# A two-layer graph network on one core: the DMAs that fold the exponentials move from SyncE's queue to ScalarE's

## The chip, the cores and the metric

The kernel runs on one core of one Trainium2 chip. The time is that of the device for one launch, in microseconds (us). The core has five engines with a stream of instructions each: TensorE (PE in the profile; its weight loads are PEld), VectorE (DVE), ScalarE (ACT), GpSimd (POOL) and SyncE (SP). A DMA is issued by an instruction in the stream of one engine, and moves its data on the core's 16 DMA engines.

## The reference

There are 128 graphs of 128 nodes each, with 256 features per node, and for each graph a matrix of zeros and ones, `adj`. Layer 0 is attention with 8 heads whose values depend on the relation, here 0 or 1, followed by a feed-forward network with GELU. Layer 1 has two steps of graph attention and a feed-forward network with ReLU. Layer norms stand between. What matters here is the attention of layer 0:

```python
scores = jnp.einsum('bhid,bhjd->bhij', q, k) / np.sqrt(dh)
attn = jax.nn.softmax(scores, axis=-1)
out = jnp.zeros_like(q)
for r in range(Wv.shape[0]):
    v_r = (src @ Wv[r] + bv[r]).reshape(Bb, Nn, h, dh).transpose(0, 2, 1, 3)
    mask = (adj_matrix == r)[:, None]
    out = out + jnp.einsum('bhij,bhjd->bhid', attn * mask, v_r)
```

The softmax needs a sum of exponentials over the source nodes for each head and each target node, and the change lies in the making of this sum.

## The kernel before, in words

**Tiling.** The 16,384 nodes are worked on in 32 groups of 512, that is 4 graphs. All data are 32-bit. In attention a group is two pairs of graphs, p = 0 and p = 1. A tile `e` holds the exponentials of a pair: the 128 partitions are source nodes, and the free dimension runs over 4 head positions `s` (4 of the 8 heads, each for two column halves `c`), the pair's 2 graphs, 2 halves and 128 targets. Each head position is one block of 128 x 512.

**The order of the work** is written out by hand. The strings FRONT, STEADY and TAIL are lists of tokens; `d:1` runs the next step of the generator `folded` for the group after the base, `a` steps attention, `f` and `k` the first and second feed-forward network, `fc` and `kc` a chain of each of them, `q` the projections, `n`, `t` norms and transposes, `l` layer 1. FRONT covers the start and parts of the first three groups, STEADY is repeated for each base group 1 to 29, and TAIL ends the run. Each engine takes its own instructions strictly in this order. So a period of the steady part holds work of several groups: pair 1 of one group's attention stands beside the second feed-forward network of the group two before.

**The steps around the change.** `scores` (L859) makes four banks of scores by matmul, and four instructions on ScalarE turn them into `e` (L866). DVE multiplies `e` by `adj` into the tile `pm` (L875). `sums` multiplies `e` and `pm` by the values, into `pav` (L929), and then multiplies the folded exponentials `es` by a constant `split` into `pden` (L917). `folded`, which the diff touches, makes `es`: for each half h of the head positions two DMAs (L891) copy, within the core's own memory (SBUF), 64 partitions by 2 blocks of 256 columns: the upper 64 source nodes of the pair's first graph go beside the lower ones of the second, and the reverse. That is 128 KB per DMA, 4 DMAs per pair, 8 per group. Then ScalarE copies the halves that stay on their partitions into a part of `pm` not yet in use (L900, two copies of 64 x 512 per h), and DVE adds both (L902). Only after that may L875 write the same part of `pm`, and the last matmuls of `pav` read it.

**The generator's steps.** The first `yield` comes after the two DMAs of h = 0, the second after those of h = 1; then one after each L900 copy and each L902. So in the list of one engine the two DMAs of one h are neighbours, and other work may stand between the two h.

**Other work named in the prediction.** In the feed-forward networks TensorE accumulates in one bank, `seeded`, that ScalarE first fills with a copy of another bank (L621, L648, L650). L629 copies `seeded` out into p16 before the next product is added to it, and L584 does the same with a bank `ph7` into p7. The step T4 of TensorE is the product that adds to `ph7` after L584. L633 and L592 are DVE's sums of these copies with banks, L549 the GELU or ReLU. L806 copies out a bank of the values' projection. L465 splits rows into planes of 16 bits, SP issues a transposing DMA of them (L468), and L493 puts the result together as `yT`. SP's queue carries also the loads of x, xT and adj (L226, L237, L223), the weights (L51), the store of the output (L1083) and a spreading of a column by way of HBM (L1008, L1009).

**Queues.** SP issues all DMAs but the first five loads of small parameters, which ScalarE issues. A wait of an instruction for more than one semaphore is carried by instructions EVENT_SEMAPHORE ahead of it in the same stream.

Of the kernel before, what the change touches and what calls it, by code (L numbers as in the profile page):

```python
# [189 lines left out]
def fast_pass(ctx, tc, a, out):  # L190
# [5 lines left out]
    nc = tc.nc  # L196
# [684 lines left out]
    def folded(S):  # L881

        n = str(S["g"])
        for p in range(G // 2):
            e = S["e", p]
            S["es", p] = es = w1p.tile([P, HC, NCH * P], F32, tag="es", name=f"es_{n}_{p}")
            for h in range(2):
                hs = slice(2 * h, 2 * h + 2)
                for lo in range(2):
                    to, fr = (slice(x * P // 2, (x + 1) * P // 2) for x in (lo, 1 - lo))  # L890
                    nc.sync.dma_start(  # L891
                        es[to, hs], e[fr, hs, lo].rearrange("p s c i -> p s (c i)")
                    )
                yield
            for h in range(2):
                hs = slice(2 * h, 2 * h + 2)
                ea = S["pm", p][:, 2 + h].rearrange("p u c i -> p u (c i)")
                for lo in range(2):
                    own = slice(lo * P // 2, (lo + 1) * P // 2)
                    nc.scalar.copy(ea[own], e[own, hs, lo].rearrange("p s c i -> p s (c i)"))  # L900
                    yield
                nc.vector.tensor_add(es[:, hs], es[:, hs], ea)  # L902
                yield
# [206 lines left out]
    with tc.manual_schedule(engines={ET.PE, ET.Activation, ET.DVE, ET.SP, ET.Pool}):  # L1110
# [29 lines left out]
        def loading(ops):  # L1140
# [11 lines left out]
        )  # L1152
        by_group = dict(
            d=folded, q=lambda S: projections(S) if S["g"] < 2 else projected(S),
            a=attention, f=first_ffn, l=layer1, k=second_ffn,
            fc=lambda S: S["chain", 1], kc=lambda S: S["chain", 3],
# [377 lines left out]
```

## Time and profile before

| what | us |
|---|---|
| median of 3 runs (2633.99 to 2634.73) | 2634.33 |
| the profiled execution | 2633.71 |
| its span, first to last instruction | 2631.9 |
| TensorE busy | 2598.8 |
| DVE busy | 2246.7 |
| ScalarE busy | 1857.4 |
| one DMA of L891 on SP, median of 256 | 0.599 |
| from issue to landing of such a DMA, median | 2.4 |
| a group in the steady part, start to start | 80.1 |

The profile is of one execution. A row of groups or of a timeline has the start, the duration, the engine, the line of the kernel, the operation, the tile written and the tile read, the shape and how often it comes in a row; behind it in square brackets the time for which the engine was idle just before, and what ended that. A name with q, such as SPq or ACTq, is the sequencer of an engine, which issues DMAs and reads semaphores; such time isn't counted as busy. TensorE's clock was granted at 0.998 of full speed over the span.

### The profile page before, as it was taken

The page shows a single profiled execution, that of the slowest core. Times are in us where ns is not written, and L with a number is a line of the kernel's source. Part 1 is how long each engine was busy: PE and PEld are TensorE (multiplying, and loading weights), DVE is VectorE, ACT ScalarE, POOL GpSimd, SP SyncE. Part 2 cuts the span into 40 slices and gives each one's busy share as a digit, 9 for nine tenths or more (in the row PEclk, how much of TensorE's full clock was granted, in tenths as well). Part 3 has the DMA queues.
Part 4 walks back from the last instruction along what each step waited for, and adds up shares of the span by engine and source line. Part 5 has one row for each costly group of instructions (what it writes and reads, how often), then busy time and mean ns, then how long its engine had stood idle before and what let it go on. Part 6 is the DMA issues. An engine that isn't in the chain of part 4 may idle for free.

```text
span 2631.9 us, 54467 instructions
## 1 busy us (share of the span) xinstructions
PE 2598.8 (99%) x20842; PEld 2302.5 (87%) x20842; DVE 2246.7 (85%) x5921; ACT 1857.4 (71%) x3839; POOL 141.8 (5%) x137
## 2 busy tenths in 40 slices
PE   8999999999999999999999999999999999999997
PEld 6888898888988988988889888889889899888886
DVE  5888888889888988888988888988889888889877
ACT  4767777667677677776776776776767777767764
POOL 0000000000000000000000000000000000000000
PEclk9999999999999999999999999999999999999999
DMA  6222232232233222222322232222323222222211
GB/s 177 69 63 61 64 66 66 53 73 65 55 67 61 65 61 65 65 66 53 75 64 59 63 67 59 63 64 65 69 53 73 61 61 65 65 57 70 60 29 34
DMA packets 317371, 170.60 MB, mean 65 GB/s; under 512 B 222768, under 2 KB 295600, under 8 KB 317104
## 3 DMA queue, kind: packets, MB, share of 16 engines
q1 hardware_dynamic: 316000, 166.66, 28.0%
q8 instruction: 166, 2.72, 0.4%
q14 instruction: 101, 0.83, 0.1%
q10 hardware_dynamic: 1104, 0.40, 0.1%
HBM read 66.20 MB, written 16.90 MB: 32 GB/s over the span
## 4 chain that ended last, share of the span: by engine, by line
PE 92%; DVE 3%; DMA 2%; ACT 2%; issue 1%; SPq 0%; POOL 0%; ACTq 0%; POOLq 0%; DVEq 0%
PE po L534 16%; PE ph L525 16%; PE seeded L525 13%; PE seeded L534 12%; PE pwo L969 4%; PE pav L929 4%; PE pw L1046 4%; PE pqqa L789 4%; PE pvqa L789 4%; PE pqqb L789 3%; PE pvqb L789 3%; PE ps L859 2%; PE py L1059 2%; PE pg L1072 2%; PE pden L917 1%; DVE x L445 1%
## 5 line engine op out<-in xcount | busy, mean ns | idle before, releaser
L465 ACT COPY planes<-x 128x512 uint16<-128x512 uint16 x384 | 227.0, 617 | 161.2 <-DVE x L445 160.5
L493 ACT COPY yT<-pT 128x512 uint16<-128x512 uint16 x384 | 268.0, 764 | 63.6 <-DMA pT<-planes 63.6
L431 POOL TENSOR_TENSOR rs<-rs,mhalf 128x4 f32<-128x4 f32 x129 | 139.5, 1081 | 2430.7 <-DVE rs L430 1836.9
L525 PE MATMUL seeded<-yS,w_L_gnn_w_ff 128*128 128x256 f32 x768 | 208.8, 394 | 2.8 <-ACT seeded L621 1.6
L866 ACT ACTIVATE e<-ps 128x512 f32<-128x512 f32 x256 | 137.0, 591 | 103.1 <-issue 89.9
L525 PE MATMUL seeded<-yS,w_L_gnn_W 128*128 128x256 f32 x768 | 204.0, 388 | 1.3 <-DVE yS L505 0.9
L525 PE MATMUL ph<-yT,w_L_gnn_w_ff 128*128 128x256 f32 x768 | 201.1, 385 | 0.5 <-ACT yT L493 0.2
L525 PE MATMUL ph<-yT,w_L_gnn_W 128*128 128x256 f32 x768 | 197.1, 380 | 0.0
L407 DVE BATCH_NORM_STATS2 st<-x 128x6 f32<-128x256 f32 x512 | 190.8, 414 | 2.4
L534 PE MATMUL po<-w_L_gnn_W,hT 128*128 128x128 f32 x1536 | 187.1, 275 | 0.5 <-ACT hT L549 0.5
L534 PEld LDWEIGHTS po<-w_L_gnn_W,hT 128*128 128x128 f32 x1536 | 184.0, 192 | 3.8 <-ACT hT L549 0.6
L534 PE MATMUL po<-w_L_gnn_w_ff,hT 128*128 128x128 f32 x1536 | 186.9, 275 | 0.0
L534 PEld LDWEIGHTS po<-w_L_gnn_w_ff,hT 128*128 128x128 f32 x1536 | 183.8, 192 | 3.4
L525 PEld LDWEIGHTS seeded<-yS,w_L_gnn_w_ff 128*128 128x128 f32 x768 | 135.7, 189 | 51.3 <-ACT p L629 16.1
L875 DVE TENSOR_TENSOR pm<-e,adj 128x512 f32<-128x512 f32 x256 | 169.7, 683 | 10.3 <-ACT e L866 9.2
L525 PEld LDWEIGHTS seeded<-yS,w_L_gnn_W 128*128 128x128 f32 x768 | 140.4, 190 | 35.2 <-ACT p L629 8.3
L633 DVE TENSOR_TENSOR hT<-seeded,p 128x512 f32<-128x512 f32 x128 | 87.6, 684 | 90.6 <-PE seeded L525 87.1
L525 PEld LDWEIGHTS ph<-yT,w_L_gnn_w_ff 128*128 128x128 f32 x768 | 143.7, 191 | 23.3 <-ACT seeded L648 0.6
L525 PEld LDWEIGHTS ph<-yT,w_L_gnn_W 128*128 128x128 f32 x768 | 143.3, 190 | 18.8 <-ACT seeded L621 0.4
L900 ACT COPY pm<-e 64x512 f32<-64x512 f32 x256 | 157.6, 616 | 2.3
L629 ACT COPY p<-seeded 128x512 f32<-128x512 f32 x128 | 75.0, 586 | 97.0 <-PE seeded L525 96.7
L549 ACT ACTIVATE hT<-hT,c_L_gnn_b_ff 128x256 f32<-128x256 f32 x256 | 112.4, 498 | 34.5 <-DVE hT L633 32.3
(195 smaller groups left out, 6399.2 us busy)
## 6 DMA issues: line engine op xcount, KB each, us to landing
es<-e SPq DMA_DIRECT2D x256, 128.0 KB, 2.4
xT<-in_xT_dram SPq DMA_DIRECT2D x32, 512.0 KB, 3.9
x<-in_x_dram SPq DMA_DIRECT2D x32, 512.0 KB, 3.9
out_dram<-x SPq DMA_DIRECT2D x31, 512.0 KB, 2.9
spread<-hbm SPq DMA_DIRECT2D x61, 256.0 KB, 4.1
adj<-in_adjT_dram SPq DMA_DIRECT2D x32, 256.0 KB, 4.4
pT<-planes SPq DMA_TRANSPOSE x192, 3.1
w_L_gnn_W<-in_L_gnn_W_dram SPq DMA_DIRECT2D x8, 256.0 KB, 5.1
```

The source lines that it names most:

```text
L407: nc.vector.bn_stats(st[:, b % 2, :], S["x"][:, b, :])
L431: nc.gpsimd.tensor_tensor(rs[:, bs], rs[:, bs], k.mhalf[:, bs], op=ALU.pow)
L465: nc.scalar.copy(planes[:, :, b], words)
L493: nc.scalar.copy(o.rearrange("p (b t h) -> p h b t", b=2, h=2), pT[:, :, :, c, :])
L525: nc.tensor.matmul(bank[:, s * TH : (s + 1) * TH], wa[:, form, 0, f * P : (f + 1) * P], m, start=start and s == 0, stop=True, skip_group_c ...
L534: nc.tensor.matmul(bank[:, s * P : (s + 1) * P], m[:, f, s * P : (s + 1) * P], wb_[:, form, f, :], start=start and s + f == 0, stop=True, ...
L549: nc.scalar.activation(o[:, s], o[:, s] if src is None else src[:, s * TH : (s + 1) * TH], func, bias=ba[:, f : f + 1],)
L789: nc.tensor.matmul(bank[:, s * TH : (s + 1) * TH], *ops, start=start and s == 0, stop=True, skip_group_check=True,)
L866: nc.scalar.activation(e[:, s], pss[s], AF.Exp, scale=SCALE)
L875: nc.vector.tensor_mul(pm[:, s], S["e", p][:, s], S["ad"][:, pair(p), None, :].to_broadcast([P, 2, NCH, P]),)
L900: nc.scalar.copy(ea[own], e[own, hs, lo].rearrange("p s c i -> p s (c i)"))
L929: nc.tensor.matmul(pav[s * DH : (s + 1) * DH, u, c, :], v[:, d0 : d0 + DH], m[:, s, u, c, :], start=(r == 0), stop=(r == 1),)
```

## The change

In `folded` the four DMAs of a pair are issued by ScalarE in place of SP. Sizes, sources, destinations and the place in the written order stay the same.

```diff
@@ -888,7 +888,7 @@
                 hs = slice(2 * h, 2 * h + 2)
                 for lo in range(2):
                     to, fr = (slice(x * P // 2, (x + 1) * P // 2) for x in (lo, 1 - lo))
-                    nc.sync.dma_start(
+                    nc.scalar.dma_start(
                         es[to, hs], e[fr, hs, lo].rearrange("p s c i -> p s (c i)")
                     )
                 yield
```

The streams of TensorE, DVE and GpSimd hold the same instructions in the same order as before. In SP's stream the 256 issues are gone. In ScalarE's stream they stand where the written order puts them. In 29 of the 32 groups it reads, for pair 0:

```
L866 (third and fourth exponential), L650, L891 x2, L806, L891 x2, L900 x4, L806
```

and for pair 1:

```
L866 (third and fourth exponential), L891 x2, L629, L891 x2, L584, L900 x2, L549 x2, L900 x2
```

The first two DMAs of a pair wait for the second exponential, the other two for the fourth. In the first two groups and the last, and in pair 0 of the third, the neighbours differ: copies of v and yh, activations of qT, or L621 stand behind the DMAs.

## The prediction

> **What bounds the kernel now.** I read the page's busy shares and its chain first, then a table of busy time by stretch, then everything at L891, then the timeline of one steady period, engine by engine.
>
> ```profile
> PE 2598.8 (99%) x20842; PEld 2302.5 (87%) x20842; DVE 2246.7 (85%) x5921; ACT 1857.4 (71%) x3839; POOL 141.8 (5%) x137
> ...
> PE 92%; DVE 3%; DMA 2%; ACT 2%; issue 1%; SPq 0%; POOL 0%; ACTq 0%; POOLq 0%; DVEq 0%
> ```
>
> ```profile
> 0.00:75.00 75.00, 65.92 (x572) 46.03 (x576) 46.48 (x127) 39.56 (x74) 3.33 (x9) 1.00 0.71 188
> ...
> 480.00:560.00 80.00, 80.00 (x649) 71.39 (x648) 69.68 (x184) 57.90 (x121) 4.21 (x5) 1.00 0.29 64
> ```
>
> TensorE (third column of the table) sets the end, and in the steady part it has no gap: one group of 512 tokens takes 80.1 us. So whatever makes TensorE wait there is paid in full; ScalarE idles 22 us per group, but only idle time in the right place can hide anything.
>
> The 256 fold DMAs are issued by SP, which nobody else waits for at that moment:
>
> ```profile
> L891 SPq DMA_DIRECT2D es<-e x256: 590/599/2017, 17.6 to 2488.2; - x128
> ```
>
> Pair 1 of a group (p = 1), where the order puts the fold among the second feed-forward's steps (start, duration, engine):
>
> ```profile
> 1283.79 0.57 ACT L621 COPY seeded<-ph 128x512 f32<-128x512 f32 x1
> 1283.87 2.76 SPq L891 DMA_DIRECT2D es<-e  x4
> ...
> 1284.27 1.09 ACT L866 ACTIVATE e<-ps 128x512 f32<-128x512 f32 x2
> ...
> 1285.63 0.59 ACT L629 COPY p<-seeded 128x512 f32<-128x512 f32 x1 [0.27 <-PE seeded L525]
> ...
> 1286.12 0.59 ACT L584 COPY p<-ph 128x512 f32<-128x512 f32 x1
> ...
> 1286.60 1.25 ACT L900 COPY pm<-e 64x512 f32<-64x512 f32 x2
> ...
> 1288.60 1.24 ACT L900 COPY pm<-e 64x512 f32<-64x512 f32 x2
> ...
> 1289.92 0.68 DVE L902 TENSOR_TENSOR es<-es,pm 128x512 f32<-128x512 f32 x1
> ...
> 1290.64 0.69 DVE L875 TENSOR_TENSOR pm<-e,adj 128x512 f32<-128x512 f32 x1
> ```
>
> See that ScalarE runs from 1285.63 without a gap until a 1.13 us pause at 1296.5, and that the second L900 copies end at 1289.84, the DVE addition L902 starts at 1289.92, and L875 after it ends at 1291.33. TensorE reaches pav<-pm (L929) at 1291.29, and the wait it carries there ends at 1291.4: this chain already stands on TensorE's edge, with no slack.
>
> **What the Trainium skill says.** "Perfetto Trace Analysis", DMA Instruction — HWDGE: the profiled time of a DMA is time of the issuing sequencer, which is free for its next instruction only at the end; the transfer comes on top. The trace agrees: SP's four stand one after the other (2.76 us for 4), and landing is 2.4 us. "Advanced Engine Details and Errata", Sequencer Loop and Engine Queue Depths: engine instructions are queued (8 deep for ScalarE) while the sequencer goes on. The trace agrees that it runs ahead; these are L866's extra semaphore waits, read at 1278.2 to 1278.3, while two copies of yT (1278.15 to 1279.56) had yet to finish ahead of them:
>
> ```profile
> L866 ACTq EVENT_SEMAPHORE  x3: 38/38/4404, 1278.2 to 1278.3; - x3
> ```
>
> "DMA: Bandwidth & Descriptors", Issuing engines are not separate DMA queues: ScalarE's and SP's DMAs share the same 16 engines, and a second issuer saves issue time alone. No run here shows a large transfer from ScalarE.
>
> **The change part by part.**
>
> *Issue time moved onto ScalarE.* 256 x 0.6 = 154 us leave SP and come to ScalarE's sequencer, 4 per pair, 8 per group. Per DMA I take 0.64 us: 0.60 and the step to the next (four back to back take 2.63 us in pair 0). ScalarE's own five issues in the first 3 us take 0.45 to 0.49, SP's loads 0.43 to 0.47, so up to a tenth more is possible: 0.60 to 0.72.
>
> *Pair 0, 29 groups: nothing.* In the new order two DMAs follow L650, then come L806 and two more, then four L900. The first needs the second exponential, which ended at 1261.7; e three and four and L650 (until 1262.98) are queued by then and run beneath it. DMAs one and two: 1261.73 to 1263.0. L806 waits for TensorE until 1263.47 anyway. DMAs three and four: to 1264.35. L900 starts at 1264.4 in place of 1263.95, and its users L902 stand at 1266.53 and 1269.58, where two copies (to 1265.7) and four (to 1266.9) are done. The cover is L806's wait and 0.8 us on DVE; were it gone, 0.45 us per group.
>
> *Pair 1, 29 groups: the cost.* New order: both last exponentials, two DMAs, L629, two DMAs, L584. DMAs one and two need the second exponential (1283.85): 1283.87 to 1285.15, under L621 and the last exponentials. L629 still starts at 1285.63, when TensorE lets it; its extra wait is read at 1285.6 in the trace, so the sequencer stands until then. Only now DMAs three and four: 1285.68 to 1286.95, with the engine at work for 0.5 us of it and then empty. Queued behind them: L584, L900, L549 and all that follows. L584 starts at 1287.0 in place of 1286.12: 0.88 late. Who waits: the TensorE step at 1287.24 (T4) needs L584 and goes at about 1287.65, 0.4 late; L900 follows 0.88 late, so the second pair ends at 1290.72, L902 starts at 1290.77, L875 ends at 1292.18, and pav<-pm goes 0.8 to 0.85 late. T4's delay lies inside that, since it is earlier on the same path. I take 0.8. ScalarE's pause at 1296.5 then takes up its lateness; TensorE's loss stays, because its 80 us have no gap. 29 x 0.8 = 23 us. Bounds: with L629 read early, DMA three could go at 1285.40 and the loss is 0.5; with 0.72 us per DMA it is 1.0. So 15 to 29 us.
>
> *First two groups and the last.* Pairs with no L629 between: copies of v, qT or seeded lie behind up to four DMAs, 1.1 us late at 19.17, 0.5 us at 2487.04. TensorE's own waits in the first 75 us amount to 9 us and give cover. Per place from -0.5 (see next) to +1.2, six places: I take 3 us, bounds -3 to 7.
>
> *SP relieved.* SP stood with loads behind it until the exponentials came (11.4 to 17.6, 26.2 to 30.7, 37.6 to 43.6 us). Those loads go earlier; but what TensorE waits for there is named as ACT and DVE, none as a load. In steady state SP's next instructions, the transposes pT at 1272.85 and 1291.0, wait for L465, not for the fold. Nothing gained; L465 itself moves with ScalarE (0.88) and is taken up by the later TensorE. Waits that become DMAs' on ScalarE for reused semaphores concern transfers issued 20 us and more before (adj, out, x): no cost. Bytes and packets are the same.
>
> Sum on the profiled execution: its time is 2633.7 (span 2631.9 and 1.8 outside), 23 + 3 = 26 gives 2659.7; the median of the runs is 0.6 above it: 2660.
>
> **Rivals.**
>
> *A: issue and engine don't overlap* (10%): a DMA goes only when ScalarE's earlier work is finished, and holds all later. Pair 1: two DMAs 1285.4 to 1286.7, L629 1.1 late, two more after it, L584 at 1288.7, 2.6 late, pav 2.4. Pair 0: L900 2.3 late, L902 1 us, TensorE 0.4. 29 x 2.8 = 81, with 5 at the ends: 2720. Against it stands the read-ahead above.
>
> *B: hidden* (9%): later engine instructions are in the queue before the DMAs hold the sequencer, or L584 is not what decides. Then only the ends cost: 2636. Against it: program order on one queue.
>
> *C: faster* (5%): the loads freed on SP shorten the start. TensorE's named waits in the first 110 us are 7.5 us; all of them gone gives 2627. It decides only if a steady group costs under 0.08 us (7.5 less 5.3, over 29). For it: DVE waited 1.9 us there for a fold that shared the DMA engines with loads.
>
> The change does move all 128 x 2 issues, in the same place of the order, so that it does nothing is no case.
>
> **How the numbers follow.** Forecast 70%, 2648 to 2675 (15 and 29 us for the steady part, -1 to +12 for ends and a tenth dearer issue). A 10%, B 9%, C 5%; the 6% left lie between 2638 and 2648 or up to 2695. Range 2635 to 2692 takes in B's value and leaves out A, C and some spread of B: under 2 in 10. A measurement tells 0.2%, 5.3 us, from no change: faster 5% (C), same 9% (B), slower 86%.
>
> **What would show it.** In the profile after: L891 as ACTq with 0.6 us each; in a steady group L629 unmoved against TensorE's step before it, then L584 about 0.9 us later behind it (now 0.49 after L629's start); pav<-pm waiting for L875; pair 0 with L806 unmoved; a period of 80.9 us. L629 moved too, or L806, means A. A period of 80.1 means B. A longer issue than 0.72 us from ScalarE, or a wait of its DMAs for DMAs of SP, would make the sum too small.

## The result, and the profile after

| | before | after |
|---|---|---|
| median (range), us | 2634.53 (2633.99 to 2635.14) | 2691.14 (2688.45 to 2693.5) |
| the profiled execution, us | 2633.71 | 2693.5 |
| its span, us | 2631.9 | 2691.7 |
| a group in the steady part, us | 80.1 | 80.9 |
| one DMA of the fold, median us | 0.599 (SP) | 0.604 (ScalarE) |

The change makes the kernel slower: after over before is 1.0215, 95% interval [1.0201, 1.0229], or 56.6 us. The forecast was 26.

**Where the time went.** Two lines of the page, busy times and the chain that ended last:

```profile
PE 2626.0 (98%) x20842; PEld 2309.5 (86%) x20842; DVE 2253.5 (84%) x5921; ACT 1863.1 (69%) x3839; POOL 141.4 (5%) x137
...
PE 89%; DVE 3%; DMA 3%; ACT 3%; ACTq 1%; issue 1%; SPq 0%; POOL 0%; DVEq 0%; POOLq 0%
```

ScalarE does no more work than before, but its sequencer (ACTq) is now on the chain with 1%, and TensorE's share fell from 92 to 89%. TensorE's busy time rose by 27 us with the same number of instructions. The windows, cut at the same VectorE instructions in both kernels (at 150.15 and 2480.16 us before), divide this rise. Of the 27 us 10.6 lie in the start, where the clock fell from 1.00 to 0.90. Another 14.6 lie in the steady part, at a clock of 1.00 in both: there a matmul behind a wait no longer overlaps the one ahead of it, so that more of its record counts as busy. The last 2 are in the last group and behind it. The windows of the two stretches shown of before:

```profile
0.00:75.00 75.00, 54.53 (x428) 35.66 (x432) 31.04 (x80) 24.78 (x46) 2.44 (x8) 0.89 0.49 132
480.00:560.00 80.00, 79.41 (x644) 70.38 (x643) 69.50 (x183) 56.99 (x118) 4.33 (x4) 1.00 0.26 64
```

In the steady stretch TensorE lost 0.6 us of 80. In the first 75 us it ran 428 matmuls in place of 572, at a clock of 0.89 in place of 1.00. To see when the lateness arises, take one VectorE instruction after the other (their order is the same in both kernels) and subtract its start before from its start after:

| VectorE's instruction, start before (us) | 17 | 28 | 36 | 50 | 70 | 120 | 150 | 2490 | 2500 | end |
|---|---|---|---|---|---|---|---|---|---|---|
| later by (us) | 0.9 | 15.5 | 17.2 | 18.0 | 28.4 | 29.3 | 32.4 | 55.7 | 58.6 | 59.8 |

So 32 us are lost in the first 150 us, 23 in 2340 us of steady work, and 4 in the last group. The steady loss is what was forecast. The other two together were forecast with 3.

**The steady part.** Pair 1 of a group, the stretch that was shown of before (timeline of all engines: start, duration, engine):

```profile
1326.01 0.60 ACTq L891 DMA_DIRECT2D es<-e  x1
...
1327.77 0.59 ACT L629 COPY p<-seeded 128x512 f32<-128x512 f32 x1 [0.27 <-PE seeded L525]
1327.79 1.26 ACTq L891 DMA_DIRECT2D es<-e  x2
...
1329.09 0.58 ACT L584 COPY p<-ph 128x512 f32<-128x512 f32 x1 [0.73 <-ACT p L629]
1329.57 1.24 ACT L900 COPY pm<-e 64x512 f32<-64x512 f32 x2
...
1332.84 0.69 DVE L902 TENSOR_TENSOR es<-es,pm 128x512 f32<-128x512 f32 x1
1333.56 0.69 DVE L875 TENSOR_TENSOR pm<-e,adj 128x512 f32<-128x512 f32 x1
```

L629 starts at 1327.77, and only then are DMAs three and four issued, at 1327.79 for 1.26 us. L584 starts 1.32 after L629 in place of 0.49, with ScalarE idle for 0.73 us: the engine waited for its own sequencer. Everything from there to L875 is 0.8 late against L629. In TensorE's own stream the distance to the kernel before is 42.13 us until the product behind L584, 42.49 there, and 42.92 from the matmul of `pav` on that needs this L875 (1291.48 before, 1334.40 now). So the wait for L584 costs 0.36 us, in part made up, and the 0.8 us is settled at `pav`.

**The start.** ScalarE at the first fold, pair 0 of group 0:

```profile
17.35 2.06 ACT L866 ACTIVATE e<-ps 128x512 f32<-128x512 f32 x4 [1.05 <-PE ps L859]
29.27 3.58 ACTq L891 DMA_DIRECT2D es<-e  x4
32.90 0.37 ACT L737 COPY v<-pv 128x256 f32<-128x256 f32 x1 [13.48 <-DMA ga<-in_L_gnn_a_dram]
```

Before, L737 started at 19.17, right behind the exponentials. Now ScalarE is idle for 13.48 us, and the releaser that the profile names is the landing of `ga`, a load of weights that SP issued and that neither L737 nor the fold uses. The four fold DMAs go from 29.27 on, nearly 10 us after their data (`e`) was complete at 19.41. What they waited for is in the built program. The completions of all DMAs of SP and ScalarE are counted on eight semaphores, handed out in turn, and a DMA waits until the one that had its semaphore before has landed. SP's and ScalarE's DMAs share the eight. In the changed kernel (user, what it waits for besides `e`, what it adds to):

```
SP  L51  temp <- b2                 adds to DMAHW0
SP  L51  g2                         adds to DMAHW1
SP  L51  gw                         adds to DMAHW2
SP  L51  ga                         adds to DMAHW3
...
ACT L891 es <- e    waits for DMAHW0 >= 80, adds to DMAHW0
ACT L891 es <- e    waits for DMAHW1 >= 80, adds to DMAHW1
ACT L891 es <- e    waits for DMAHW2 >= 80, adds to DMAHW2
ACT L891 es <- e    waits for DMAHW3 >= 80, adds to DMAHW3
```

Two of them on SP's queue:

```profile
21.38 0.33 SPq L51 DMA_DIRECT2D temp<-in_L_gnn_b_dram  x1
...
22.84 0.47 SPq L51 DMA_DIRECT2D ga<-in_L_gnn_a_dram  x1
```

All four loads were issued after `e` was ready; `temp` landed 7.8 us later, at 29.2, `ga` 9.4 us later, at 32.2. The records of the trace name the semaphore of each DMA and bear this out: the loads ahead of the four folds on their semaphores landed at 29.19, 30.06, 30.77 and 32.23, and the folds were issued at 29.27, 30.08, 30.84 and 32.26. Before the change SP stood in front of the fold until `e` came, so all loads behind it were also behind it in the turn of the semaphores. With the fold gone from SP its loads run ahead of it, and the fold on ScalarE inherits their semaphores. The same happens at the second pair of group 1, whose `e` was complete at 82.15:

```profile
85.30 0.57 ACT L621 COPY seeded<-ph 128x512 f32<-128x512 f32 x1 [3.15 <-DMA temp<-in_L_gnn_b_ff_dram]
...
87.25 3.21 ACTq L891 DMA_DIRECT2D es<-e  x2
90.50 0.62 ACT L900 COPY pm<-e 64x512 f32<-64x512 f32 x1 [4.62 <-DMA w_L_gnn_w_ff<-in_L_gnn_w_ff_dram]
```

The pair's four DMAs were issued at 80.33, 84.66, 87.25 and 89.86. Ahead of them on their semaphores a transposing DMA of SP had landed at 80.30, and loads at 84.64, 87.17 and 89.83.

TensorE's largest waits, over the whole span (us in total, times, longest), show both places and the steady wait for L584, 29 times (the rest of the steady loss, at `pav`, is not among them):

```profile
PE pav L929 <- ACT v L737: 8.1, 1, 8.1
PE ph L525 <- ACT p L584: 6.7, 29, 0.6
...
PE ph L525 <- ACT seeded L621: 3.2, 1, 3.2
```

And the clock falls behind such gaps. Two windows of after (PE, PEld, DVE, ACT, POOL, clock, DMA share, GB/s); before the change the clock was 1.00 in both:

```profile
33.00:46.00 13.00, 6.47 (x104) 4.68 (x104) 6.78 (x16) 4.40 (x10) 0.00 (x0) 0.60 0.25 58
...
80.00:92.00 12.00, 3.82 (x14) 2.35 (x12) 1.44 (x5) 3.88 (x8) 0.72 (x1) 0.68 0.93 234
```

At 46.77 the sixteen matmuls of one projection (L719) take 8.83 us in place of 7.13, although the gap just ahead of them is 1.69 us in both kernels. So a part of the loss is paid later than the long waits; which of them brings it about was not shown.

### The profile page after: what moved, and what is told of

It reads as the page before. It is cut to its first block, busy times and chain, and to the rows that moved or that the text cites. A ratio compares the mean times of both kernels' runs of the same rounds, so it can differ in the third digit from the quotient of the medians.

```text
span 2691.7 us, 54401 instructions
## 1 busy us (share of the span) xinstructions
PE 2626.0 (98%) x20842; PEld 2309.5 (86%) x20842; DVE 2253.5 (84%) x5921; ACT 1863.1 (69%) x3839; POOL 141.4 (5%) x137
## 4 chain that ended last, share of the span: by engine, by line
PE 89%; DVE 3%; DMA 3%; ACT 3%; ACTq 1%; issue 1%; SPq 0%; POOL 0%; DVEq 0%; POOLq 0%
PE po L534 16%; PE ph L525 16%; PE seeded L534 12%; PE seeded L525 12%; PE pav L929 5%; PE pwo L969 4%; PE pw L1046 4%; PE pqqa L789 4%; PE pvqa L789 4%; PE pqqb L789 3%; PE pvqb L789 3%; PE ps L859 2%; PE py L1059 2%; PE pg L1072 2%; PE pden L917 1%; ACTq L891 1%
## 5 line engine op out<-in xcount | busy, mean ns | idle before, releaser
L525 PE MATMUL ph<-yT,w_L_gnn_w_ff 128*128 128x256 f32 x768 | 207.3, 393 | 7.8 <-ACT p L584 6.7
L525 PE MATMUL seeded<-yS,w_L_gnn_W 128*128 128x256 f32 x768 | 207.2, 393 | 4.7 <-DVE yS L505 4.7
L525 PE MATMUL seeded<-yS,w_L_gnn_w_ff 128*128 128x256 f32 x768 | 207.3, 392 | 3.2 <-ACT seeded L621 3.1
L525 PE MATMUL ph<-yT,w_L_gnn_W 128*128 128x256 f32 x768 | 199.0, 382 | 3.2 <-ACT seeded L621 3.2
L525 PEld LDWEIGHTS ph<-yT,w_L_gnn_w_ff 128*128 128x128 f32 x768 | 139.6, 191 | 50.3 <-ACT p L584 18.3
L900 ACT COPY pm<-e 64x512 f32<-64x512 f32 x256 | 157.6, 615 | 35.2 <-ACT pv L806 20.1
L875 DVE TENSOR_TENSOR pm<-e,adj 128x512 f32<-128x512 f32 x256 | 169.9, 684 | 11.2 <-ACT e L866 10.1
L525 PEld LDWEIGHTS seeded<-yS,w_L_gnn_W 128*128 128x128 f32 x768 | 142.3, 192 | 39.1 <-ACT p L629 8.3
L525 PEld LDWEIGHTS seeded<-yS,w_L_gnn_w_ff 128*128 128x128 f32 x768 | 138.4, 190 | 42.8 <-ACT p L629 16.1
L525 PEld LDWEIGHTS ph<-yT,w_L_gnn_W 128*128 128x128 f32 x768 | 144.4, 192 | 22.4 <-ACT seeded L621 3.6
L629 ACT COPY p<-seeded 128x512 f32<-128x512 f32 x128 | 75.0, 586 | 95.2 <-PE seeded L525 94.8
```

The source lines that it names most:

```text
L525: nc.tensor.matmul(bank[:, s * TH : (s + 1) * TH], wa[:, form, 0, f * P : (f + 1) * P], m, start=start and s == 0, stop=True, skip_group_c ...
L875: nc.vector.tensor_mul(pm[:, s], S["e", p][:, s], S["ad"][:, pair(p), None, :].to_broadcast([P, 2, NCH, P]),)
```

## The experiments

The theory: (1) in the steady part only the two issues behind L629 in pair 1 cost, by holding ScalarE's sequencer; (2) in the start ScalarE stands for loads of SP whose semaphores its DMAs take over; (3) a few us are issue time at the remaining places. The rivals: ScalarE's issue time, or its use as an issuer as such, makes all of it, in proportion to the DMAs; or the loads that run ahead disturb the start by themselves. Differences below are to the median of the kernel before, measured beside it.

**The change split in start and rest.** In both, F stands for the pairs of groups 0 and 1 and pair 0 of group 2:

```diff
-                    nc.scalar.dma_start(
+                    (nc.sync if F else nc.scalar).dma_start(    # e1_start_back
+                    (nc.scalar if F else nc.sync).dma_start(    # e2_start_only
```

> The fold's DMAs of groups 0 and 1 and of pair 0 of group 2 go back to SyncE; the other 29 + 29 pairs and the last stay on ScalarE. Theory (the start loses 33 us because ScalarE's DMAs stand there for loads of SyncE; the steady part loses 0.8 us a group; the end 3 to 4): 2634.5 + 23 + 4 = 2661 to 2662, period 80.9. Rival (the lateness of the start merely shows where later work of the run is pushed, and the loss is spread over ScalarE's use as an issuer): 56.6 x 57/64 pairs, 2685.

> The complement: only the fold's DMAs of groups 0 and 1 and of pair 0 of group 2 (20 of 256) are issued by ScalarE. Theory: the whole loss of the start without the rest, 2634.5 + 33 = 2667 to 2668, period 80.1. Rival (loss by issue time): 20 x 0.64 us can cost 13 us at most, 2636 to 2648.

Measured: with the start back on SP 2660.72, +28.0 us, ratio 1.0103 [1.0088, 1.0119]; with the start alone on ScalarE 2662.37, +29.7, ratio 1.0109 [1.0093, 1.0124]. The first is 1 us over the 27 that the theory had added, the second 3 under its 33. The two halves add to 57.7, the whole change is 56.6. Twenty DMAs cost 29.7 us, 1.5 us each where an issue takes 0.6: more than their issue time, so it can't be in proportion. In the second kernel VectorE is late by 15.4 us after the first pair, 1.7 more after the second, 0.8 after the third, 9.4 after the fourth (pair 1 of group 1) and 1.2 after the fifth. Two places hold 25 of them.

**SP held in the start, as it was before.** The whole change, with 8 bytes of `e` read by SP where the fold stood:

```diff
+                if n in "01":
+                    nc.sync.dma_start(seen[:, 2 * h : 2 * h + 2], e[:1, hs, 1, 1, P - 1])
                 for lo in range(2):
```

> The whole change, all 256 DMAs on ScalarE, but in groups 0 and 1 SyncE is kept standing for the exponentials as before, by 8 DMAs of 8 bytes that read e into a tile which nobody uses. So SyncE's loads don't run ahead, and the completion semaphores that ScalarE's DMAs take over are those of earlier transfers. Theory: the start's loss goes but for some issue time, 2634.5 + 23 + 4 + 3 to 5 = 2664 to 2668. Rival (ScalarE's own issue time, or what lies behind the DMAs on it, makes the loss of the start): 2685 to 2692.

Measured: 2680.32, +47.6, ratio 1.0174 [1.016, 1.0188]. The theory missed by 12 to 16 us, and the rival's value was not reached either. ScalarE's timeline tells why (L895 and L904 are L891 and L900 here, four lines further down):

```profile
21.34 0.37 ACT L737 COPY v<-pv 128x256 f32<-128x256 f32 x1 [1.80 <-issue]
...
34.03 4.43 ACTq L895 DMA_DIRECT2D es<-e  x3
38.50 0.69 ACT L724 ACTIVATE qT<-pq,c_L_gnn_bq 128x512 f32<-128x512 f32 x1 [4.16 <-DMA es<-e]
```

At the first place the hold did what it should: ScalarE is idle for 1.80 us, put down to issue, where it was 13.48, and VectorE is late by 2.0 to 2.7 us behind it in place of 14 to 16. At the second place it did not: three DMAs stretch over 4.43 us, since the last of them takes over the semaphore of a load of `adj` that SP issued at 34.02 and that landed at 37.81; it was issued at 37.83. And the hold itself has a price, as SP's loads now come late: TensorE waits 3.0 us for c_L_gnn_b (L349), where its wait for the same was 0.6 in the kernel before. In all VectorE is still late by 21 us at the instruction where it was 32. So the run settles the first place, and not the sum.

**The fold of the start on GpSimd.** Its DMAs count on semaphores of their own in the built program:

```diff
+                    (nc.gpsimd if F else nc.sync).dma_start(
```

> Groups 0 and 1 and pair 0 of group 2 fold by DMAs of GpSimd, which share no completion semaphore with SyncE's and hold no other engine; all others on SyncE. SyncE's loads run ahead here too. Theory (the loss needs ScalarE standing for loads): 2633 to 2638, no loss. Rival (loads that run ahead disturb the start in themselves, by filling the DMA engines ahead of the folds): 2650 to 2668.

Measured: 2636.95, +4.3, ratio 1.0015 [1.0008, 1.0021]. SP's loads run ahead of the fold here just as in the changed kernel, and 25 of the 30 us are not lost. So loads that run ahead cost no more than these 4.3 us by themselves; they also gain nothing. The cost arises at the first place: the four DMAs of the fold land 6.2 to 7.2 us after their issue there, where it was 2.4 to 4.7 before, and the addition behind them (L902) is 4.1 us late.

**Standing without folding.** The kernel with the fold of the start on GpSimd, and beside it one DMA of 8 bytes from ScalarE at each of the ten places:

```diff
+                if n in "01" or n == "2" and not p:
+                    nc.scalar.dma_start(seen[:, 2 * h : 2 * h + 2], e[:1, hs, 1, 1, P - 1])
                 for lo in range(2):
```

> As the run with the start's folds on GpSimd (2637), but ScalarE issues one DMA of 8 bytes, that reads e and is used by nobody, at each of the ten places where it issued two of the fold. They take over semaphores of SyncE's loads. Theory: ScalarE stands for the loads although hardly anything is issued, most of the loss comes back: 2652 to 2665. Rival (issue time, size of the transfers): ten issues of under 0.5 us, 2637 to 2642.

Measured: 2649.41, +15.4, ratio 1.0057 [1.0043, 1.0071], 11 more than without the small DMAs and 3 below the theory's lower end. Most of it arises at the first place, where VectorE becomes 12.4 us late, 8.7 more than without the small DMAs:

```profile
29.72 1.86 ACTq L892 DMA_DIRECT2D seen<-e  x2
31.62 0.37 ACT L737 COPY v<-pv 128x256 f32<-128x256 f32 x1 [13.54 <-DMA seen<-e]
```

Two DMAs of 8 bytes (L892) hold ScalarE for 13.54 us, as long as four DMAs of 128 KB. So at this place it is neither the size nor the number, but the semaphore: the two were issued at 29.72 and 31.01, behind loads on their semaphores that landed at 29.64 and 29.98. At the fourth place only about 1 us came back: with two DMAs in place of four the turn falls there on a transposing DMA, for which ScalarE's own next copy waits too, and on a load that lands soon after the data is ready.

**The loads moved, the fold on ScalarE.** To have the fold on ScalarE without sharing semaphores with the loads, the loads behind the first fold are issued by GpSimd; a companion has the fold on SP.

```diff
-                queue.dma_start(t, src)
+                (self.nc.gpsimd if self.moved else queue).dma_start(t, src)
```

(`moved` is set at the first fold; x, xT and adj of groups 0 to 2 go the same way.)

> As the run with only the start on ScalarE (20 DMAs of groups 0 and 1 and of pair 0 of group 2), but the loads of SyncE that come after the first fold in the written order, up to group 2, are issued by GpSimd. ScalarE's DMAs then take over the semaphores of transfers that are long done, while the loads run ahead as in the changed kernel. Theory, corrected after the first four runs (of the 30 us of the start some 20 are ScalarE standing for loads, the rest is issue time of 2.6 to 3 us at a place where four DMAs stand together): its companion with the folds on SyncE plus 5 to 13 us, 2638 to 2650. Rival (issue time and what stands behind it make nearly all): the companion plus 25 to 30, 2657 or more.

> The companion of the run before: the same loads on GpSimd, all folds on SyncE. A base for it, and a look at whether loads that are not held by the folds gain anything: 2630 to 2640 by both theories; under 2628 if TensorE's waits in the start were the loads' doing.

Measured: fold on ScalarE 2660.12, fold on SP 2661.15 (+26.1 and +27.1; ratios 1.0097 [1.0082, 1.0113] and 1.01 [1.0085, 1.0116]). The companion missed its forecast by over 20 us: with the loads on GpSimd TensorE waits for the first weights and later for their users, whatever the fold does. But the difference between the two is what was asked for. The theory had 5 to 13 us for it and the rival 25 to 30; it is -1.0 us in the medians and at most 2.8 in the shifts of the traces (at the fourth place under 1), so both had too much. On a start so disturbed some cost may be hidden. Still, 20 fold DMAs on ScalarE cost 29.7 us when they take over the semaphores of loads on the way, and here, where the loads ahead of the first four had landed 5.7 us and more before, next to nothing was seen.

**The changed kernel with two places taken out.** 248 DMAs stay on ScalarE:

```diff
+                    (nc.gpsimd if n + str(p) in ("00", "11") else nc.scalar).dma_start(
```

> The changed kernel with 8 of its 256 DMAs, those of pair 0 of group 0 and pair 1 of group 1, on GpSimd and the other 248 on ScalarE. Theory (at these two places ScalarE stood for loads, 15 and 9 us of the 30): what is left of the start is 4 for GpSimd's folds and 2 to 6 of issue time, 2634 + 27 + 6 to 10 = 2667 to 2671. Rival (each place in the start costs alike): 2691 less 2 of 5 places, 2679.

Measured: 2668.87, +34.2, ratio 1.0132 [1.0117, 1.0148], as the theory had it. Eight DMAs of 256 carry 22 of the 57 us.

**The steady part, taken apart.** From group 2's pair 1 on, only the two DMAs of h = 1 of pair 1 on ScalarE; then all but these:

```diff
+                    (nc.scalar if p and h and S["g"] > 1 else nc.sync).dma_start(     # e8_pair1_second
+                    (nc.sync if F or (p and h) else nc.scalar).dma_start(             # e9_rest_of_steady
```

> Only the two DMAs of h = 1 of pair 1 from group 2 on are issued by ScalarE (60 of 256), all others by SyncE. Theory (the steady loss is L584 and all behind it held by exactly these two issues): 2634 + 23 + 0 to 3 for the last group = 2656 to 2660, period 80.9. Rival (each DMA on ScalarE costs alike): 23 x 60/236 = 6, 2640.

> The steady part without the two DMAs of the run before: pair 0 whole and h = 0 of pair 1 are issued by ScalarE (from pair 1 of group 2 on), h = 1 of pair 1 and the start by SyncE. Theory (pair 0 and the first two of pair 1 run beneath waits for TensorE and exponentials that are there anyway): no steady loss, 2634 to 2638 with up to 3 for the last group, period 80.1. Rival (each DMA on ScalarE costs alike): 17, 2651.

Measured: the two of pair 1 alone 2657.94, +23.9, ratio 1.009 [1.0074, 1.0105], period 80.93. The rest 2637.89, +3.2, ratio 1.0013 [1.0006, 1.0019], period 80.13, and VectorE loses 2.9 of it between 2490 and 2500 us, in the last group. Start, these two and the rest add up: 29.7 + 23.9 + 3.2 = 56.8.

The last group, in the second of them (ScalarE, then TensorE, then windows, whose third number from the end is TensorE's clock):

```profile
2486.84 1.26 ACTq L891 DMA_DIRECT2D es<-e  x2
2488.15 1.08 ACT L866 ACTIVATE e<-ps 128x512 f32<-128x512 f32 x2 [1.33 <-issue]
```

```profile
2489.77 0.88 PEld L525 LDWEIGHTS seeded<-yS,w_L_gnn_w_ff 128*128 128x128 f32 x4 [3.45 <-ACT seeded L621]
2489.78 1.60 PE L525 MATMUL seeded<-yS,w_L_gnn_w_ff 128*128 128x256 f32 x4 [3.05 <-ACT seeded L621]
```

```profile
2491.00:2492.00 1.00, 1.00 (x3) 0.74 (x3) 0.74 (x2) 0.90 (x2) 0.00 (x0) 0.50 0.72 171
2492.00:2493.00 1.00, 1.00 (x4) 0.79 (x3) 0.65 (x1) 0.00 (x0) 0.00 (x0) 0.50 0.47 95
...
2494.00:2496.00 2.00, 2.00 (x11) 1.77 (x10) 0.71 (x2) 1.83 (x5) 0.00 (x0) 1.00 0.03 8
```

Here the order puts the two DMAs between the second and the third exponential, where nothing is queued on the engine. The third is 1.33 us late, TensorE's wait for `seeded` grows from 1.61 to 3.05 us, and then the matmuls behind it run at half the clock until 2494: four of L525 take 1.91 us in place of 1.03. A hold of 1.3 us became 2.9. The Trainium skill, "TensorE: Matmul & The Clock Gate", What's actually happening, says that the clock is halved after an idle window of about 3.4 us and comes back after a busy one, and that the windows run freely. The trace agrees with the halving (0.50) and with its length (0.73 on average from 2489.7 to 2491, 0.50 to 2493, 0.64 to 2494, so some 3.5 us). The gap before it was 3.05 us by the records of the matmuls, whose ends are modelled, and 3.45 by those of the weight loads, so this run doesn't tell whether a gap shorter than the page's window is enough.

**How long the hold is.** Of the two DMAs one goes back to SP; in another kernel both stay, but L584's step is written ahead of them:

```diff
+                    (nc.scalar if p and h and lo and S["g"] > 1 else nc.sync).dma_start(   # e10_one_of_two
-... kc:-1*2 a:1 n1:0 d:1 k:-1 d:1 a:1 d:1 a:1*3 ...
+... kc:-1*2 a:1 n1:0 k:-1 d:1 d:1 a:1 d:1 a:1*3 ...                                     # e11_after_L584
```

> Of the two DMAs of h = 1 of pair 1 only the second is issued by ScalarE, the first by SyncE. Theory: the sequencer is held from L629's start for one issue of 0.6 in place of two, L584 is 0.24 late in place of 0.88, so 0.2 a group, 4 to 7 us: 2638 to 2642. Rival (the loss is one of being held at all, or half for half the DMAs): 12, 2646, or more.

> The two DMAs of h = 1 of pair 1 on ScalarE, but the written order has L584's step ahead of them, so they are held by nothing but L629 and L584 in the queue and hold L900. Theory: L584 on time; the DMAs run from about 1285.7 to 1287.0 beneath L629 and L584, L900 starts 0.4 late in place of 0.8: 29 x 0.4 = 12 us, 2645 to 2649. Rival (the loss is L900 and DVE's addition waiting for a fold that lands late): as with the order before, 2656 to 2660, or more since the fold is issued later.

Measured: one of two 2639.36, +4.7, ratio 1.0016 [1.001, 1.0023], period 80.27; both behind L584 2644.66, +10.0, ratio 1.0043 [1.0029, 1.0056], period 80.47. The first is as the theory had it, the second at the lower end of its 2645 to 2649. The second kernel's ScalarE:

```profile
1288.13 0.59 ACT L629 COPY p<-seeded 128x512 f32<-128x512 f32 x1 [0.27 <-PE seeded L525]
1288.18 0.60 ACTq L891 DMA_DIRECT2D es<-e  x1
1288.62 0.59 ACT L584 COPY p<-ph 128x512 f32<-128x512 f32 x1
...
1289.48 1.25 ACT L900 COPY pm<-e 64x512 f32<-64x512 f32 x2 [0.27 <-issue]
```

L584 is on time, 0.49 after L629, since it was queued before the DMAs; L900 starts 1.35 after L629 in place of 0.97. So the loss is the issue time that sticks out beyond the work queued ahead of it. Behind one copy (0.49 us) one issue of 0.6 cost 0.14 us a group, a half of the DMAs and a sixth of the loss, and two issues of together 1.27 cost 0.8; behind two copies (0.97 us) the two cost 0.34.

None of these kernels beats the kernel before; those that come within 5 us of it are the ones that keep ScalarE out of the costly places, or leave it a single issue there.

## Why the prediction was wrong

**Pair 1, 29 groups x 0.8 = 23 us: right,** in size and in mechanism. Period 80.93 for a forecast of 80.9, L584 late against L629 by 0.83 for 0.88, TensorE by 0.36 for 0.4 at the product behind it (T4) and by 0.79 for 0.8 at `pav`, and the two DMAs alone cost 23.9 us, of which about 1 is the last group's. Its competitor A (issue and engine work exclude each other) is refuted by the fold's first two DMAs, which run at 1326.01 and 1326.64 while ScalarE computes, and B (hidden) by the period.

**Pair 0: nothing. Right in the sum, wrong in the detail.** DMAs three and four were put beneath L806's wait for TensorE. The trace of after:

```profile
1305.61 0.59 ACT L806 COPY pv<-pvqa 128x512 f32<-128x512 f32 x1 [0.49 <-PE pvqa L789]
1305.67 1.26 ACTq L891 DMA_DIRECT2D es<-e  x2
1306.97 2.52 ACT L900 COPY pm<-e 64x512 f32<-64x512 f32 x4 [0.77 <-ACT pv L806]
```

They are issued only when L806 has started: here a DMA did not pass an instruction ahead of it that still waited for its semaphore. In pair 1 the prediction had reckoned with just that, at L629. L900 starts 1.36 us after L806 in place of 0.48, so it is 0.88 late where 0.45 was forecast, and the cover held all the same (L902 stands unmoved): the second L806, at 1310.85, waits 1.37 us for TensorE (2.25 before), and the run with pair 0 on ScalarE has a period of 80.13.

**"First two groups and the last ... I take 3 us, bounds -3 to 7": this step failed.** It measured 32 + 4 us in the profiled executions. It counted issue time, less a small gain from loads that go earlier, and no wait. What broke it is a sentence further down, under SP relieved: **"Waits that become DMAs' on ScalarE for reused semaphores concern transfers issued 20 us and more before (adj, out, x): no cost."** In the steady part that is so: behind 150 us no DMA of the fold was issued less than 19.9 us after the one ahead of it on its semaphore had landed. In the start the transfers are loads issued 2 to 4 us *after* the fold's data was ready, because the fold no longer keeps SP back. The first part of the same paragraph had the piece in hand ("Those loads go earlier") and asked only whether someone gains by it, not whose semaphores they then occupy. At the first place the semaphore is shown to be the cause (8 bytes hold ScalarE as long, and with SP held the place costs 2.0 to 2.7). At the fourth place each DMA was issued within 0.1 us of the landing ahead of it on its semaphore, ScalarE stood idle until then for 3.15 and 4.62 us, and taking the place out gives its loss back. Some 4 us of the first place are not the wait, but folds that land later beside the loads, as the run with the fold on GpSimd suggests; and up to 10 us of the 32 are matmuls made longer by the lower clock, for which the working had no price either.

That the measured 2691 still lies within the stated range of 2635 to 2692 is luck. The terms of the sum reached no further than 2675, and what stands between that and 2692 was no allowance for this wait.

**The size of what was known.** In the last group the hold was seen ("0.5 us at 2487.04") and measured 1.33, since the exponentials stand behind the DMAs, not only L621; TensorE's lower clock behind the gap doubled it.

**Competitor C (the loads freed on SP gain up to 7.5 us): refuted.** With the fold of the start on GpSimd the loads are as free, and the kernel is 4.3 us slower, not faster.

The last sentence of the prediction named the case ("a wait of its DMAs for DMAs of SP would make the sum too small"), with no number. The order of ScalarE's and SP's DMAs in the changed program was there to be read, and would have shown which loads the fold waits for.

## What to carry to other kernels

Before moving a DMA from a queue that only moves data to one that computes, ask what the old queue will do when it is no longer held, and which semaphores the moved DMA shares with it: its wait for them now stops an engine. Then price the issue time only where it sticks out beyond the work already queued on the new engine, and from there follow it to the bound engine. A place where everything waits for the same few loads is priced by itself, not by the mean of the steady part.

## What had not been expected of the hardware

- A DMA on ScalarE was issued no earlier than the instruction ahead of it started, where that one waited for a semaphore: 1305.67 behind an L806 at 1305.61, 1327.79 behind an L629 at 1327.77, and by the same 0.06 and 0.02 us in all 29 groups. Behind instructions that only waited for their turn on the engine it went at once (1288.18 to 1289.44 over L629 and L584).
- A gap of TensorE was paid a second time in places: 0.50 of the clock for some 3.5 us behind a gap of 3.05, 0.60 over the 13 us around the waits of 8.1 and 4.4. Behind a gap of 1.61 at the same place of the kernel before it stayed at 1.00. Behind one of 1.69 it stayed at 1.00 before the change and fell after it (the projection at 46.77), so these runs give no length from which it begins.
- The landing of small loads in the start (128 and 256 KB) took 7.8 and 9.4 us, while the DMA engines were busy for 0.78 of the time (20 to 33 us); a fold DMA in the same stretch took up to 7.2, where its median is 2.4.
